# A 192-wide context split as 128 + 64 instead of 128 + 65: one column folded into the weights, and the second part of the weighted sum kept in two halves of the array's columns

## The chip, the cores and the metric

The kernel runs on one core of a Trainium2 chip. The metric is the device time of one execution in microseconds. A core has a matrix engine (TensorE, PE in the profile, with its weight loads shown as PEld), a vector engine (VectorE, DVE), a scalar engine (ScalarE, ACT), GpSimd (POOL) and the queue that issues most of the DMAs (SyncE, SP). Matmul results land in PSUM; ACT and DVE copy them to SBUF. Everything here is in fp32.

## The reference

Cross attention followed by a mixture of experts, for 32 sequences of 100 tokens (256 wide), each with its own context of 361 rows (192 wide). Cut to what matters:

```python
x1 = layernorm(_layernorm(x), ln1_g, ln1_b)         # 32 x 100 x 256
x2 = layernorm(ctx_768, ln2_g, ln2_b)               # 32 x 361 x 192
q, k, v = x1 @ Wq + bq, x2 @ Wk + bk, x2 @ Wv + bv  # 256 wide
attn = softmax(einsum('bqe,bke->bqk', q, k) * 256 ** -0.5)
x = x + einsum('bqk,bke->bqe', attn, v) @ Wo + bo
h = _layernorm(x)
# 31 experts, top 3 of each token, and one shared expert, each 256 -> 256 -> 256 with gelu
x = x + h + shared(h) + sum of gate * expert(h) over the token's three experts
```

A normalised context row, before the gain `ln2_g` and the offset `ln2_b`, is (row - mean) / sigma, so its 192 entries add up to zero (but for rounding). The change rests on this.

## The kernel before, in words

Keys and values are never formed. The query side and the key weights are folded into one 256 x 193 matrix `m_sb` (`fold_scores`, L337), so that the scores of a sequence are `qk` times the normalised context. The 193rd column stands for the constant part of the keys. The weighted sum over keys is taken of the normalised context itself (`weighted`, L523) and only then multiplied by the folded value and output weights `wvo` (`fold_values`, L357, and `project_out`, L539). The context tile `z` has a column of ones behind its 192 columns (`zring`, L137 to L140), which carries the bias row of `wvo` and the softmax denominator.

So the 193 columns (192 and the ones) are worked in two parts, listed as (part, first column, columns) in `AUG` (L304):

```python
C2 = D2 - P            # 64
A2 = C2 + 1            # 65
AUG = [(0, 0, P), (1, P, A2)]
```

The attention is one loop over 32 sequences with some more turns for the lag of later steps (L840 to L935). PE, DVE, ACT, POOL and SP take their instructions in exactly the order in which the loop writes them (`manual_schedule`, L83). In turn i the matrix engine is given, in this order:

- the transposes of the exponentials of sequence i-2 (`exp_transpose`, tile `pe`, L514),
- the scores of sequence i-1 (`scores`, tile `pss`, L495), first the part of 128 context columns, then the part of 65,
- the transposes of a token tile for the router (`route_turn`, tile `pl`, L642),
- the transposes of the context of sequence i (`ctx_transpose`, tile `pz`, L487), three for each part,
- the counts of the router (`route_count`, tile `pp`, L697 and L698),
- the weighted sums of sequence i-2 (`weighted`, tile `pcx`, L528): for each of the two parts three key chunks (128, 128 and 105 keys) are added up in PSUM,
- the router's logits (`pr`, L649), the query projection of a token tile (`token_project`, tile `pq`, L455, the two parts again), a transpose of the next one (`px`, L446) and the output projection (`project_out`, tile `po`, L544).

An fp32 matmul is two instructions on the engine (each with a weight load of its own), a transpose is one. There are 25 token tiles of 128 tokens for 32 sequences, so the steps that go by token tile are missing in some turns. ACT copies each result out: `z2T` (L488), `qk` (L459), `exT` (L515 and L520) and `cT` (L535); DVE takes the row maximum `nm` (L500), and ACT the exponentials `ex` (L506). DVE also normalises the context (L231) and takes its statistics (L246).

Before the loop (the first 15 us), Wq and Wk are transposed on PE (`transposed`, L306, copied by ACT), the seven vectors are turned into columns (`vectors`, L293), two bias columns are made (`bias_cols`, L317), and the folded matrices follow. Wv is transposed in turn 1 and `fold_values` runs in turn 2.

Behind the loop, DVE works out the places of the routed tokens in some thirty small steps (L951 to L1026), while PE does four parts of the shared expert (`shared_mm`, L782); the 92 expert slots follow (`run`, L1167), and a tail that collects and stores the results.

Which part of the 128 x 128 array a matmul uses is worked out from its operands when the program is built: with over 64 rows and over 64 columns of weights it is the full array. With 64 or fewer rows, or columns, it is a tile of 64 (with 32 or fewer, of 32) rows or columns, and the other tiles of the array can then be used by other instructions. The program before has few such places: 64-row tiles in `transposed` and `bias_cols` for Wk and Wv, 32-row tiles in the shared expert's biases (`shared_bias`, L775, and `shared_biases`, L371), and three transposes into 32-column tiles (`p_ec`, L993, and `p_oh`, L997).

Of the kernel before, what the change touches and what calls it, by code (L numbers as in the profile page):

```python
# [15 lines left out]
ET = mybir.EngineType  # L16
PSUM = bass.MemoryType.PSUM


# [19 lines left out]
def xattn_ffn(  # L39
# [18 lines left out]
    C2 = D2 - P  # L58
    A2 = C2 + 1
    DA = D2 + 1  # L60
# [61 lines left out]
    pool.memset(vrows[:8, :], 0.0)  # L122
    pool.memset(vrows[:8, D2:DA], 1.0)

# [48 lines left out]
    load_w(wo_sb, Wo, nc.sync)  # L173
    bo_t = prep_t(1, D1)[:, 0, :]
    nc.sync.dma_start(bo_t[C2:A2, :], bo[None, :])

# [126 lines left out]
    NEC = E // P  # L303
    AUG = [(0, 0, P), (1, P, A2)]  # L304

    def transposed(w_sb, kd, dst, name):  # L306

        rows = sum(m for _, m in kd)
        for ec in range(NEC):
            pt = ps_t(f"pt_{name}{ec}")  # L310
            for c, m in kd:
                nc.tensor.transpose(
                    pt[:, c * P : c * P + m], w_sb[:m, c, ec * P : (ec + 1) * P], ident[:m, :m]
                )
            nc.scalar.copy(dst[:, ec, :rows], pt[:, :rows])

    def bias_cols(w_sb, kd, ln_b, bias, dst, name):  # L317
# [9 lines left out]

    wqT, wkT, wvT = (prep_t(NEC, n) for n in (D1, DA, DA))
    bqc = att.tile([P, NEC], F32, tag="bqc", name="bqc")
    m_sb = att.tile([P, 2, DA], F32, tag="m", name="m_sb")  # L330
# [6 lines left out]
    def fold_scores():  # L337
        for c in range(2):
            pm = ps_m(f"pm{c}")
            for ec in range(NEC):  # L340
                nc.tensor.matmul(
                    pm[:, :DA], wqT[:, ec, c * P : (c + 1) * P], wkT[:, ec, :],
                    start=(ec == 0), stop=(ec == NEC - 1),
                )
            nc.scalar.activation(m_sb[:, c, :], pm[:, :DA], AF.Copy, scale=g1s[:, c : c + 1])
        for c, s, m in AUG:
            pc = ps_m(f"pc{c}")
            for ec in range(NEC):
                nc.tensor.matmul(
                    pc[:m, :1], wkT[:, ec, s : s + m], bqc[:, ec : ec + 1],  # L350
                    start=(ec == 0), stop=(ec == NEC - 1),
                )
            nc.vector.tensor_scalar(
                c_sb[:m, c : c + 1], pc[:m, :1], vcol[:m, c, G2 : G2 + 1], SC, ALU.mult, ALU.mult
            )

    def fold_values():  # L357
        for c, s, m in AUG:
            pw = ps_m(f"pw{c}")
            for ec in range(NEC):  # L360
                nc.tensor.matmul(
                    pw[:m, :D1], wvT[:, ec, s : s + m], wo_sb[:, ec, :],
                    start=(ec == 0), stop=(ec == NEC - 1),
                )
            nc.scalar.activation(wvo[:m, c, :D1], pw[:m, :D1], AF.Copy, scale=vcol[:m, c, G2 : G2 + 1])
        nc.vector.tensor_tensor(wvo[C2:A2, 1, :D1], wvo[C2:A2, 1, :D1], bo_t[C2:A2, :], ALU.add)
        nc.vector.memset(wvo[C2:A2, 1, D1 : D1 + 1], 1.0)

# [34 lines left out]
    transposed(wq_sb, KD1, wqT, "q")  # L403
    transposed(wk_sb, KD2, wkT, "k")
    ctx_stats(0)
    ctx_rough(0)
    vectors()
    for t in XG[0]:
        token_stats(t)
    token_rough(0)  # L410
    bias_cols(wq_sb, KD1, B1, BQ, lambda ec: bqc[:, ec : ec + 1], "bqc")
    bias_cols(wk_sb, KD2, B2, BK, lambda ec: wkT[:, ec, D2:DA], "bkc")
    ctx_rstd(0)
    token_rstd(0)
# [35 lines left out]
    def token_project(t):  # L450
# [7 lines left out]
        for c, s, m in AUG:  # L458
            nc.scalar.activation(  # L459
                qk[:m, c, t * P : (t + 1) * P], pq[:m, c * P : (c + 1) * P], AF.Identity,  # L460
                bias=c_sb[:m, c : c + 1], scale=vcol[:m, c, G2 : G2 + 1],
            )
# [60 lines left out]
    def weighted(b):  # L523
        z, exT = ztile.pop(b), att_eT.pop(b)
        for a, s, m in AUG:
            pw = ps_m(f"pcx_{b}_{a}")
            for c, (_, n) in enumerate(CH):
                nc.tensor.matmul(  # L528
                    pw[:m, :L1], z[:n, c, s : s + m], exT[:n, c, :], start=(c == 0), stop=(c == NCH - 1)
                )  # L530
            q = 0
            while q < L1:
                col = (b * L1 + q) % RING
                n = min(L1 - q, RING - col)
                nc.scalar.copy(cT[:m, a, col : col + n], pw[:m, q : q + n])  # L535
                q += n


    def project_out(t):  # L539
        k, j = divmod(t, TPB)  # L540
        xt = xb[k][:, j, :]
        po = ps_m(f"po_{t}")
        for a, _, m in AUG:
            nc.tensor.matmul(  # L544
                po[:, : D1 + 1], cT[:m, a, t * P % RING : t * P % RING + P], wvo[:m, a, :], start=(a == 0), stop=(a == 1)
            )
# [293 lines left out]
    for i in range(B + 5):  # L840
# [80 lines left out]
        if i == 1:  # L921
            transposed(wv_sb, KD2, wvT, "v")
            bias_cols(wv_sb, KD2, B2, BV, lambda ec: wvT[:, ec, D2:DA], "bvc")
# [13 lines left out]
    shared_half(1, 1, ps_m)  # L937
    for t in range(2):
        shared_mm(t)
# [65 lines left out]
    for t in range(2):  # L1005
        shared_add(t)
    shared_mm(2)
    PACK, BITS = 4, 5
# [287 lines left out]
```

## Time and profile before

| what | value |
|---|---|
| time, median of 3 runs | 476.42 us (474.83 to 476.57) |
| time of the profiled execution | 475.09 us |
| its span, first to last instruction | 473.2 us |
| attention loop, first scores to last scores | 17.1 to 211.8 us, so 6.28 us a turn |
| experts and tail | from about 240 us on |
| PE busy over the span | 451.0 us (95%) |
| DVE, ACT, POOL busy | 311.0 (66%), 252.3 (53%), 254.0 us (54%) |

The busy time of PE in the profile counts each matmul from its issue to the modelled end of its results, and matmuls overlap in the pipeline; what one costs is better read from the distance between the starts of two that follow each other. In the timeline rows below, the columns are the start in us from the start of the span, the time that the row covers, the engine, the line, the operation, output<-inputs, the shape (rows*columns of the array in front), and the number of instructions that were merged into the row. A row that was asked for with a narrow window holds only the instructions in that window.

### The profile page before, as it was taken

The page shows a single profiled execution, that of the slowest core. Times are in us where ns is not written, and L with a number is a line of the kernel's source. Part 1 is how long each engine was busy: PE and PEld are TensorE (multiplying, and loading weights), DVE is VectorE, ACT ScalarE, POOL GpSimd, SP SyncE. Part 2 cuts the span into 40 slices and gives each one's busy share as a digit, 9 for nine tenths or more (in the row PEclk, how much of TensorE's full clock was granted, in tenths as well). Part 3 has the DMA queues.
Part 4 walks back from the last instruction along what each step waited for, and adds up shares of the span by engine and source line. Part 5 has one row for each costly group of instructions (what it writes and reads, how often), then busy time and mean ns, then how long its engine had stood idle before and what let it go on. Part 6 is the DMA issues. An engine that isn't in the chain of part 4 may idle for free. (4 is left out here: it accounts for less than half of the span.)

```text
span 473.2 us, 10916 instructions
## 1 busy us (share of the span) xinstructions
PE 451.0 (95%) x2978; PEld 389.2 (82%) x2978; DVE 311.0 (66%) x1273; ACT 252.3 (53%) x839; POOL 254.0 (54%) x523
## 2 busy tenths in 40 slices
PE   8899999898999999999799999999999999999996
PEld 8687887777888788887478999999999999997564
DVE  2679998998999896867764444444444455655177
ACT  2565877787877787774514444444444444443210
POOL 6322486887676757575803555554655555556200
PEclk9979999999999999999999999999999999999999
DMA  6987954454545741021269988898798899962593
GB/s 188 272 223 216 278 168 126 140 161 148 160 130 155 230 165 65 35 82 58 91 181 289 317 257 253 264 274 256 239 279 269 268 365 353 355 247 71 185 408 131
DMA packets 65863, 98.79 MB, mean 209 GB/s; under 512 B 8289, under 2 KB 40616, under 8 KB 65800
## 3 DMA queue, kind: packets, MB, share of 16 engines
q1 hardware_dynamic: 56360, 72.60, 51.6%
q0 software_dynamic: 8768, 24.79, 13.8%
q8 instruction: 28, 0.46, 0.4%
q10 hardware_dynamic: 672, 0.66, 0.4%
q14 instruction: 35, 0.29, 0.2%
HBM read 68.27 MB, written 29.74 MB: 207 GB/s over the span
## 5 line engine op out<-in xcount | busy, mean ns | idle before, releaser
L566 POOL DMA_INDIRECT y_d<-ys,yrow x92 | 90.3, 982 | 96.2 <-ACT ys L1139 42.4
L1123 ACT ACTIVATE hT<-ph,b1t 128x128 f32<-128x128 f32 x184 | 57.6, 364 | 102.6 <-issue 53.2
L1118 PE MATMUL ph<-xgT,w 128*128 128x128 f32 x736 | 101.9, 282 | 1.0 <-DVE xgT L1110 1.0
L1118 PEld LDWEIGHTS ph<-xgT,w 128*128 128x128 f32 x736 | 94.7, 197 | 1.5 <-DVE xgT L1110 1.4
L1133 PE MATMUL py<-w2r,hT 128*128 x368 | 94.3, 380 | 0.0
L566 POOL DMA_INDIRECT xs_d<-xl,su x75 | 75.1, 1002 | 30.7 <-ACT cT L535 13.0
L1133 PEld LDWEIGHTS py<-w2r,hT 128*128 128x128 f32 x368 | 62.9, 190 | 4.8
L1141 DVE TENSOR_SCALAR ys<-py,gate 128x256 f32<-128x256 f32 x46 | 22.3, 484 | 61.3 <-PE py L1133 40.8
L1110 DVE COPY xgT<-pg 128x256 f32<-128x256 f32 x92 | 38.1, 420 | 28.0 <-PE pg L1108 28.0
L495 PE MATMUL pss<-z2T,qk 65*100 65x361 f32 (+1 forms) x128 | 46.2, 483 | 0.8 <-ACT qk L459 0.6
L528 PE MATMUL pcx<-exT,z 128*65 128x100 f32 (+3 forms) x384 | 45.3, 268 | 0.0
L528 PEld LDWEIGHTS pcx<-exT,z 128*65 128x65 f32 (+3 forms) x384 | 40.6, 168 | 0.7 <-ACT er L675 0.7
L1108 PEld LDWEIGHTS pg<-ident,xg 128*128 128x128 f32 x184 | 35.4, 195 | 4.2
L1108 PE MATMUL pg<-ident,xg 128*128 128x128 f32 x184 | 35.5, 277 | 0.0
L246 DVE BATCH_NORM_STATS2 stc<-z 128x6 f32<-128x192 f32 (+1 forms) x96 | 27.8, 345 | 7.0 <-DMA z<-in_ctx_dram 7.0
L455 PE MATMUL pq<-zT,m_sb 128*128 128x128 f32 (+1 forms) x200 | 28.2, 284 | 2.1 <-DVE eq L711 1.2
L544 PE MATMUL po<-wvo,cT 128*128 128x257 f32 (+1 forms) x100 | 27.4, 394 | 2.7 <-ACT cT L535 2.4
L506 ACT ACTIVATE ex<-pss,nm 100x361 f32<-100x361 f32 x32 | 18.0, 563 | 20.6 <-DVE nm L500 17.1
L495 PEld LDWEIGHTS pss<-z2T,qk 65*100 65x100 f32 (+1 forms) x128 | 19.2, 170 | 11.2 <-ACT qk L459 1.5
L1139 ACT ACTIVATE ys<-py,gate 128x256 f32<-128x256 f32 x46 | 21.8, 475 | 11.7 <-issue 8.8
L487 PE MATMUL pz<-ident,z 128*128 128x128 f32 (+2 forms) x192 | 26.2, 271 | 1.1 <-PE pss L495 0.9
L487 PEld LDWEIGHTS pz<-ident,z 128*128 128x128 f32 (+2 forms) x192 | 22.4, 143 | 5.1 <-PE pss L495 1.5
(242 smaller groups left out, 826.1 us busy)
## 6 DMA issues: line engine op xcount, KB each, us to landing
w<-in_L_ffn_We_dram SPq DMA_DIRECT2D x92, 256.0 KB
xg<-xs_d SPq DMA_DIRECT2D x92, 131.5 KB
w2r<-in_L_ffn_We_dram SPq DMA_DIRECT2D x31, 256.0 KB
z<-in_ctx_dram SPq DMA_DIRECT2D x32, 192.0 KB
y<-y_d SPq DMA_DIRECT2D x13, 384.0 KB
ye<-y_d SPq DMA_DIRECT2D x12, 384.0 KB
xs_d<-none SPq DMA_DIRECT2D x3, 1052.0 KB
x<-in_x_dram SPq DMA_DIRECT2D x5, 512.0 KB
```

What stands on the lines that cost most here:

```text
L246: nc.vector.bn_stats(st[:n, c, :], ztile[b][:n, c, :D2])
L455: nc.tensor.matmul(pq[:m, c * P : (c + 1) * P], m_sb[:, d, s : s + m], z[:, d, :], start=(d == 0), stop=(d == 1))
L487: nc.tensor.transpose(pt[:m, ks : ks + n], z[:n, c, s : s + m], ident[:n, :n])
L495: nc.tensor.matmul(pss[:L1, :L2], qk[:m, a, b * L1 : (b + 1) * L1], z2T[:m, a, :], start=(a == 0), stop=(a == 1),)
L528: nc.tensor.matmul(pw[:m, :L1], z[:n, c, s : s + m], exT[:n, c, :], start=(c == 0), stop=(c == NCH - 1))
L544: nc.tensor.matmul(po[:, : D1 + 1], cT[:m, a, t * P % RING : t * P % RING + P], wvo[:m, a, :], start=(a == 0), stop=(a == 1))
L566: ins = nc.gpsimd.indirect_dma_start(out=dst, out_offset=bass.IndirectOffsetOnAxis(ap=index, axis=0), in_=src, in_offset=None).ins
L1108: nc.tensor.transpose(pt[:, c * P : (c + 1) * P], g[:, c::2], ident)
L1110: nc.vector.tensor_copy(xgT[i].rearrange("p c s -> p (c s)"), pt[:, : 2 * P])
L1118: nc.tensor.matmul(ph[:, f * P : (f + 1) * P], w1s[:, c, f::2], z[:, c, :], start=(c == 0), stop=(c == 1))
L1123: nc.scalar.activation(hT[i][:, f, :], ph[:, f * P : (f + 1) * P], AF.Gelu, bias=b1t[:, f, i : i + 1])
L1133: nc.tensor.matmul(py[:, :D1], h[:, f, :], w2f[:, bass.ds(e * (2 * D1) + f * D1, D1)], start=(f == 0), stop=(f == 1),)
```

## The change

Because a normalised row adds up to zero, its first entry is minus the sum of the others. A product with a vector w over 192 columns is therefore a product with w - w[0] over the last 191. So the first context column is dropped from every product and put into the weights: `with_gains` multiplies Wk and Wv by `ln2_g`, `without_first` transposes and subtracts the first column. The 191 columns and the ones make 192 = 128 + 64, and `AUG` becomes `[(0, 1, 128), (1, 129, 64)]`.

With 64 columns the second part fits into half of the array's columns. In `weighted` its key chunks 0 and 2 are added up on PSUM partitions 0 to 63 and chunk 1 on partitions 64 to 127. `cT` and `wvo` then have 128 rows for the second part too, `wvo` with the same 64 rows twice, so that `project_out` adds the two halves. The bias row of `wvo` goes in through an extra matmul of one row (`last_row`, `bo_t`). One part of the shared expert (`shared_mm(2)`) moves from behind the router's placement steps to in front of them.

In the program that this makes, the following use a tile of the array instead of the whole: the second part of `pz` (3 transposes a turn), of `pq` (4 instructions for a token tile) and of `pcx` (6 instructions a turn) use 64-column tiles, of `pcx` one key chunk in the upper one; the second part of `pss` (4 instructions a turn) uses a 64-row tile. The order of the steps in the loop is the same, and the order of SP's DMAs is unchanged.

```diff
-    pool.memset(vrows[:8, D2:DA], 1.0)
...
-    bo_t = prep_t(1, D1)[:, 0, :]
-    nc.sync.dma_start(bo_t[C2:A2, :], bo[None, :])
+    bo_t = prep_t(2, D1).rearrange("p n c -> p (n c)")
+    nc.sync.dma_start(bo_t[:1, :D1], bo[None, :])
+    pool.memset(bo_t[:1, D1 : D1 + 1], 1.0)
+    pool.memset(bo_t[:1, D1 + 1 : D1 + C2], 0.0)
+    pool.memset(bo_t[:1, D1 + C2 : D1 + C2 + 1], 1.0)
+    last_row = bo_t[:1, D1 + 1 : D1 + 1 + C2]
...
-    AUG = [(0, 0, P), (1, P, A2)]
+    AUG = [(0, 1, P), (1, 1 + P, C2)]
...
+    def with_gains(w_sb, dst):
+        for c, m in KD2:
+            nc.vector.tensor_scalar(dst[:m, c, :], w_sb[:m, c, :], vcol[:m, c, G2 : G2 + 1], None, ALU.mult)
+
+    def without_first(w_sb, dst, name):
+        for ec in range(NEC):
+            pt = ps_t(f"pt_{name}{ec}")
+            for c, m in KD2:
+                nc.tensor.transpose(
+                    pt[:, c * P : c * P + m], w_sb[:m, c, ec * P : (ec + 1) * P], ident[:m, :m]
+                )
+            nc.vector.tensor_copy(dst[:, ec, :1], pt[:, :1])
+            nc.vector.tensor_scalar(dst[:, ec, 1:D2], pt[:, 1:D2], dst[:, ec, :1], None, ALU.subtract)
...
     def fold_values():
...
+        pw = ps_m("pw1")
+        for h in range(2):
+            half = pw[h * C2 : (h + 1) * C2, :]
+            nc.tensor.matmul(half[:, : D1 + 1], last_row, bo_t[:1, : D1 + 1], start=True, stop=False)
             for ec in range(NEC):
                 nc.tensor.matmul(
+                    half[:, :D1], wvT[:, ec, 1 + P : DA], wo_sb[:, ec, :], start=False, stop=(ec == NEC - 1)
                 )
-        nc.vector.tensor_tensor(wvo[C2:A2, 1, :D1], wvo[C2:A2, 1, :D1], bo_t[C2:A2, :], ALU.add)
-        nc.vector.memset(wvo[C2:A2, 1, D1 : D1 + 1], 1.0)
+        nc.scalar.copy(wvo[:, 1, :], pw[:, : D1 + 1])
...
     transposed(wq_sb, KD1, wqT, "q")
-    transposed(wk_sb, KD2, wkT, "k")
     ctx_stats(0)
     ctx_rough(0)
     vectors()
+    with_gains(wk_sb, wkg)
...
     bias_cols(wk_sb, KD2, B2, BK, lambda ec: wkT[:, ec, D2:DA], "bkc")
+    without_first(wkg, wkT, "k")
...
                 qk[:m, c, t * P : (t + 1) * P], pq[:m, c * P : (c + 1) * P], AF.Identity,
-                bias=c_sb[:m, c : c + 1], scale=vcol[:m, c, G2 : G2 + 1],
+                bias=c_sb[:m, c : c + 1],
...
         for a, s, m in AUG:
             pw = ps_m(f"pcx_{b}_{a}")
             for c, (_, n) in enumerate(CH):
+                h = c % 2 if a else 0
+                last = c + (2 if a else 1) >= NCH
                 nc.tensor.matmul(
-                    pw[:m, :L1], z[:n, c, s : s + m], exT[:n, c, :], start=(c == 0), stop=(c == NCH - 1)
+                    pw[h * C2 : h * C2 + m, :L1], z[:n, c, s : s + m], exT[:n, c, :], start=(c == h), stop=last
                 )
...
-                nc.scalar.copy(cT[:m, a, col : col + n], pw[:m, q : q + n])
+                nc.scalar.copy(cT[:, a, col : col + n], pw[:, q : q + n])
...
-        for a, _, m in AUG:
+        for a in range(2):
             nc.tensor.matmul(
-                po[:, : D1 + 1], cT[:m, a, t * P % RING : t * P % RING + P], wvo[:m, a, :], start=(a == 0), stop=(a == 1)
+                po[:, : D1 + 1], cT[:, a, t * P % RING : t * P % RING + P], wvo[:, a, :], start=(a == 0), stop=(a == 1)
             )
...
         if i == 1:
-            transposed(wv_sb, KD2, wvT, "v")
+            with_gains(wv_sb, wvg)
+            without_first(wvg, wvT, "v")
...
-    for t in range(2):
+    for t in range(3):
         shared_mm(t)
...
-    shared_mm(2)
```

## The prediction, made before the changed kernel had run

> **What bounds the kernel now.** I read the page first, for the engine that is full, then busy time by window over the attention loop, because only the loop and what stands ahead of it are changed, then PE's timeline of one turn, and last PE's waits there.
>
> ```profile
> PE 451.0 (95%) x2978; PEld 389.2 (82%) x2978; DVE 311.0 (66%) x1273; ACT 252.3 (53%) x839; POOL 254.0 (54%) x523
> PEclk9979999999999999999999999999999999999999
> ...
> 45.00:70.00 25.00, 24.28 (x180) 20.50 (x179) 23.47 (x112) 19.00 (x70) 14.21 (x30) 1.00 0.85 227
> 120.00:145.00 25.00, 23.96 (x178) 20.41 (x176) 23.30 (x105) 18.99 (x72) 17.48 (x33) 1.00 0.48 142
> ...
> 57.84 1.46 PE L495 MATMUL pss<-z2T,qk 128*100 128x361 f32 x4
> 59.14 0.39 PE L642 MATMUL pl<-ident,xl 128*128 128x128 f32 x2
> 59.36 0.79 PE L487 MATMUL pz<-ident,z 128*128 128x128 f32 x6
> 59.99 0.32 PE L697 MATMUL pp<-sums,onesf 128*128 128x31 f32 x2
> 60.17 1.41 PE L528 MATMUL pcx<-exT,z 128*128 128x100 f32 x12
> 61.42 0.55 PE L649 MATMUL pr<-wr,qk 128*128 128x31 f32 x4
> ```
>
> In the windows the columns are the length, then busy us of PE, PEld, DVE, ACT and POOL, the granted clock, the DMA share and GB/s. PE is at 24 of 25 us at full clock, DVE close behind at 23.4, ACT at 19. From start to start in the turn at 57.84: four score instructions take 1.30 us, of which the first pays for its own weights, so about 302 ns each; six transposes take 0.63 us, 108 ns each; the twelve of pcx take 1.25 us. The single starts show two speeds in these twelve: 112 ns in the first part (128-column weights) and 86 ns in the second (65 columns). So a weight load of 128 columns takes about 107 ns, and 100 moving columns about 84 ns, and each instruction costs the longer of the two, since the next load runs beside the matmul. For 64 columns I put the load at 54 ns, half of 107; for 100 columns at 84.
>
> PE's waits, from the view of who waits for whom between 40 and 215 us (total, times, longest):
>
> ```profile
> PEld po L544 <- ACT cT L535: 5.0, 10, 1.2
> PEld pr L649 <- ACT ex L506: 4.5, 5, 1.1
> PEld pq L455 <- DVE eq L711: 1.4, 2, 0.7
> ```
>
> With four smaller ones for pq (issue 0.7, ex 0.4, pr 0.3) and some for pss and pz, PE waits about 17 us of 175. PE is the bound, with some 0.6 us of waiting in a turn of 6.28 us.
>
> **The change: what a tile of the array costs.** The program before changes between the whole array and a part of it in few places, and they show the price:
>
> ```profile
> 9.64 0.30 PEld L322 LDWEIGHTS bkc<-vcol,w2r 128*128 128x128 f32 x2
> 9.96 0.29 PEld L322 LDWEIGHTS bkc<-vcol,w2r 64*128 64x128 f32 x2
> 10.27 0.30 PEld L322 LDWEIGHTS bkc<-vcol,w2r 128*128 128x128 f32 x2
> ...
> 441.58 0.59 PE L750 MATMUL phs<-qk,ws_sb 128*128 128x512 f32 x1
> 442.10 0.18 PEld L780 LDWEIGHTS pys<-b,gT 32*128 32x128 f32 x1 [0.75 <-issue]
> ...
> 50.92 0.38 PE L544 MATMUL po<-wvo,cT 65*128 65x257 f32 x1
> 51.23 0.31 PEld L374 LDWEIGHTS pb<-ident,b1r 32*128 32x128 f32 x2 [0.33 <-PE po L544]
> ```
>
> Loads of one kind in bqc and bkc follow each other at 112 ns, so a pair takes 0.22 us; each pair here takes 0.31 to 0.32, since the next pair is on another tile. At 441.58 the 512 columns stream for 428 ns (the distance of those matmuls), to 442.01; the load for the 32-row tile starts at 442.10, 90 ns later, where elsewhere it starts beside the matmul. At 50.92: 257 columns, 216 ns, to 51.14; load at 51.23, again 90 ns. Leaving a tile shows the same (pys to 442.66, next load 442.75). The transposes of Wv (23.03 and 23.29) leave 46 ns. So at a change of tile nothing overlaps: matmul, a pause D of 90 ns (46 between transposes), load, matmul. The cost of one change is the last matmul + D + the next load, less the longer of matmul and load.
>
> [...]
>
> In each turn, in ns:
> - pss, second part, 64-row tile, between 361-column matmuls: in, 90 + 84 = 174; out to pl or pz, 90 + 107 = 197. 371 x 32 turns = 11.9 us.
> - pz, second part, 64-column tile: in, 88 + 46 + 54 - 88 = 100; out to pp or pcx, 88 + 46 + 107 - 107 = 134. 234 x 32 = 7.5 us.
> - pcx: in, 84 + 90 + 54 - 84 = 144; out to pr, pq or px, 84 + 90 + 107 - 107 = 174. 318 x 32 = 10.2 us. The two column halves can overlap: the four 32-row tiles of pys start 7 ns apart (the starts from 442.11), each with its own load. Chunk 1 then runs beside chunks 0 and 2, so 4 x 86 instead of 6 x 86: minus 172 x 32 = 5.5 us.
> - pq, by token tile: in, 107 + 90 + 54 - 107 = 144; out, 197. 341 x 25 = 8.5 us.
>
> Sum: 11.9 + 7.5 + 10.2 - 5.5 + 8.5 = 32.6 us of PE time. No row shows a change from the whole array to a column tile and back that isn't hidden in a wait; the nearest is p_oh, a 32-column tile, whose successor's load came 81 ns after its stream. So I price column tiles as row tiles; the bounds are 0 (then only pss's 11.9 - 5.5 = 6.4 us remains) and the 90 ns taken.
>
> Do transposes in a column tile stay single? [...] The two p_ec transposes, with one weight column and so in such a tile, start at 234.43 and 234.54, 108 ns apart like whole ones. [...]
>
> **What the waits take back.** The time is put ahead of pr, pq and po, and these wait now for ACT and DVE work that starts earlier on PE (ex after pss, cT after pcx). Their waits, 5.0 + 4.5 + 2.8 = 12.3 us in 175, are 14 us in the loop's 200. All of it at most, none at least; I take 13, since the switches out of pss and in pz, some 0.4 us, come between pss and pr, and pq's 0.34 ahead of po. DVE doesn't take over: it has some 5.9 us of work in a turn that grows to 6.9. Loop: 32.6 - 13 = +19.6 us.
>
> **Ahead of the loop.** wkT was ready at 11.36 (last bkc sum). Now PE turns the vectors first, DVE scales Wk (two of 256 columns, 433 ns each by the L231 row of that shape), bias sums end near 10.8, the four transposes of Wk (0.95 us before) come behind them, and DVE does two copies of a column (158 ns, the L326 row) and two subtractions of 191 columns from PSUM (about 0.4, below the 484 of the 256-column L549). fold_scores starts near 12.3 instead of 11.1. Behind these on DVE wait the statistics' factors and the normalising of context 0, so ACT's first zx moves too: +1.0 us, none if the turns at 8.6 us that follow absorb it. Wv in turn 1: two scalings and four small steps, 2 us of DVE where ACT had two copies; fold_values gets two one-row matmuls of 257 columns (four instructions of 215 ns), a second set of 64 columns, and changes of tile, less a DVE add (0.4) that waited 2.4: together +1.0, from 0 to 3.
>
> **Costed at nothing.** cT for 128 rows (both row counts take 234 to 247 ns), po with 128 rows (216 ns apart either way), qk without a scale (ACT has 6 us idle in 25, and ACT's 457 ns don't change), three POOL memsets (0.1 us each, POOL is done with its set-up by 5.9 and wanted at 8.2), SP's queue (no DMA is added or moved). shared_mm(2), 4 x 215 ns, leaves the place behind the biases, where the next PE step waits for ACT's ohT (ended 238.25), and enters PE's 0.8 us of waiting ahead of p_ec at 234.43: delay of p_ec up to 0.3, and its reader eT waited until 237.9 for pys. Nothing; at most 0.3 either way.
>
> **The sum.** 19.6 + 2 = +21.6 on the profiled execution's 475.1 (span 473.2 and 1.9 around it): 496.7. That execution is 1.3 us below the median of 476.42, within the spread shown. I say 496.
>
> **The rivals.**
> A, above, 0.74: every change of tile drains. from +12 us (the pauses of column tiles at half, 6.6 us less, all 14 us of waits taken back, no set-up) to +33 (no wait taken back): 487 to 508.
> B, 0.12: only row tiles drain, column tiles change for nothing. 11.9 - 5.5 + 2, less what the waits take: -3 to +8, so 473 to 483, near 477. For it: no clean row of a column tile. [...]
> C, 0.08, faster: the drains fall into PE's waits altogether. 3.8 round trips of a turn cost less than what the waits take (13/32 = 0.41) and the halves give (0.17), less set-up 0.06: it decides at 0.52/3.8 = 140 ns for a round trip. With none priced, the 5.5 us of the halves remain: about 471. Against: the cheapest round trip above, bkc's, is already 0.18, and pss's 0.37.
> D, 0.06: the change doesn't do what it says; the halves don't overlap (+5.5) or transposes there double (+10). 502 to 515.
>
> **How the numbers follow.** Half a per cent, 2.4 us, is about what a measurement of this kernel can tell from no change. Slower: nearly all of A and D and a third of B, 0.83. Same: half of B and a sliver of A, 0.07. Faster: C and some of B, 0.10. The range for 8 in 10 is 480 to 508: it leaves out C, most of B and the upper half of D, 0.2.
>
> **What would show it.** In the profile after: turns of about 6.9 us instead of 6.28; PE starts 170 to 200 ns further apart at pss's second part and behind it, 100 to 150 at the second parts of pz, pcx and pq, with the next weight load behind the matmul's stream; chunk 1 of pcx starting within some 20 ns of chunk 0; the waits for ex and cT nearly gone. I am wrong if loads into column tiles start beside the last matmul of the whole array, or if the waits stay beside longer PE work (then up to 508).

## The result, and the profile after

The changed kernel takes 494.89 us (median of 6 runs, 493.40 to 495.57), the kernel before 475.62 us beside it (6 runs, 472.46 to 477.14): a ratio of 1.0414, 95% interval 1.0370 to 1.0459. The prediction had said slower, 496 us. The total is right; where the time sits is not where the prediction put it. Ratios here and below are of undisturbed executions; one profile, that of `filled`, was taken of a disturbed one, and no time is read from it.

The profiled execution took 495.5 us, span 493.7. First the page of the changed kernel: busy time by engine, and the granted clock in 40 slices of the span.

```profile
PE 476.7 (97%) x2986; PEld 385.7 (78%) x2986; DVE 314.9 (64%) x1283; ACT 247.3 (50%) x835; POOL 252.3 (51%) x525
PEclk9666999999999999999989999999999999999999
```

PE has 25.7 us more busy time for eight more instructions; the other engines are within 5 us of what they had. In the clock row three slices (12.3 to 49.4 us) stand at 6 where before they stood at 9, 7 and 9. This is the first sign of something the prediction has no term for. The 7 of the kernel before is a stretch at half clock too, in turns 1 and 2; its windows there show a clock of 0.53 and 0.62:

```profile
24.00:28.00 4.00, 4.00 (x13) 2.79 (x13) 3.81 (x21) 2.78 (x9) 0.36 (x2) 0.53 1.00 198
28.00:32.00 4.00, 4.00 (x25) 3.86 (x24) 3.58 (x18) 2.19 (x6) 2.33 (x4) 0.62 1.04 343
```

Next the busy time by window, columns as before (length, PE, PEld, DVE, ACT, POOL, clock, DMA share, GB/s): first one stretch in the middle of the loop of the changed kernel, then all turns from the third scores to the last, of the kernel before and of the changed one.

```profile
120.00:145.00 25.00, 25.00 (x174) 18.69 (x172) 22.46 (x102) 19.87 (x75) 17.45 (x35) 1.00 0.48 142
```

```profile
34.46:211.82 177.36, 168.43 (x1236) 143.06 (x1234) 154.15 (x689) 137.49 (x505) 116.55 (x235) 1.00 0.50 150
```

```profile
47.96:232.44 184.48, 183.44 (x1235) 134.90 (x1234) 153.99 (x683) 133.82 (x505) 114.52 (x233) 1.00 0.46 143
```

The middle stretch holds 174 PE instructions where the kernel before had 178, and PE stands nowhere in it. Over the 29 turns PE's idle time fell from 8.9 us (177.36 - 168.43) to 1.0, and the turns grew by 7.1 us, 6.12 to 6.36 us each. That is a third of the whole difference. The 177.35 of the kernel before is on the long side: in the profiles of `mm2`, `wide_before`, `warm_before` and `warm_two` below, whose loop is the same, these turns take 175.6 to 176.6 us, while `gains_top`, `wide_after` and `warm_after`, with the changed loop, take 184.4 to 184.5. So the change costs 7 to 9 us in these turns. The starts of the scores split the span:

| us of the profiled execution | before | after | difference |
|---|---|---|---|
| start to first scores | 17.08 | 20.42 | +3.3 |
| turns 1 and 2 | 17.38 | 27.54 | +10.2 |
| 29 turns, third to last scores | 177.35 | 184.48 | +7.1 |
| last scores to the end | 261.43 | 261.27 | -0.2 |

So 13.5 us of the 20.5 arise in the first 48 us. Now the timeline of one turn of the changed kernel, PE alone, to set beside the turn at 57.84 of the kernel before:

```profile
59.51 1.55 PE L522 MATMUL pss<-z2T,qk 128*100 128x361 f32 x4
60.99 0.51 PE L672 MATMUL pl<-ident,xl 128*128 128x128 f32 x2
61.33 0.79 PE L514 MATMUL pz<-ident,z 128*128 128x128 f32 x6
61.96 1.32 PE L558 MATMUL pcx<-exT,z 128*128 128x100 f32 x12
63.20 0.63 PE L679 MATMUL pr<-wr,qk 128*128 128x31 f32 x4
63.67 1.27 PE L482 MATMUL pq<-zT,m_sb 128*128 128x128 f32 x8
```

From start to start the scores take 1.48 us (1.30 before) and the pl behind them 0.34 (0.22). The six transposes pz take 0.63 us, exactly what they took before, though three of them are in the 64-column tile. The twelve of pcx take 1.24 us against 1.25.

The single starts give the price of a change of tile, in the form in which the prediction worked it out:

| per turn, ns | at the way in | at the way out | sum | predicted |
|---|---|---|---|---|
| pss (second part 64 rows) | 91 + 82 | 92 + 111 | 376 | 371 |
| pz (second part 64 columns) | 0 | 0 | 0 | 234 |
| pcx (halves of columns) | 92 + 53 | 91 + 81 | 317 | 318 |
| pq (64 columns) | 94 + 51 | 94 + 56 | 295 | 341 |

Each pair is the excess of two starts that follow each other over what the same two take without a change, the pause and then the load that nothing covers; the medians over all turns from 50 us on agree within 5 ns. In pcx chunk 1 starts 7 ns behind chunk 0 (62.712 and 62.719), and the six instructions of the second part take four steps.

Who waits for whom, PE alone from 48 to 210 us, of the changed kernel:

```profile
PE po L574 <- ACT cT L565: 0.6, 1, 0.6
PE pz L514 <- ACT qk L673: 0.2, 1, 0.2
```

PE's waits for ex (3.5 us in that window before) and for eq (1.2) are gone and that for cT is halved (1.2 before), much as the prediction said. Last the timeline of turn 1 in the changed kernel: one line of PE, and the DVE line that it waits for.

```profile
29.62 1.45 PE L332 MATMUL pt_v<-ident,w2r 128*128 128x128 f32 x4 [5.29 <-DVE w2r L325]
31.00 2.12 PE L343 MATMUL bvc<-vcol,w2r 128*128 128x1 f32 x8
```

```profile
29.06 0.18 DVE L211 BATCH_NORM_AGGREGATE mv<-st_x 128x2 f32<-128x6 f32 x1
29.16 0.57 DVE L325 TENSOR_SCALAR w2r<-w2r,vcol 128x256 f32<-128x256 f32 x2
```

PE stands 5.29 us ahead of the transposes of Wv, because `with_gains(wv_sb, wvg)` is queued on DVE behind the statistics of contexts and tokens of that turn. Before, these transposes took Wv as it had been loaded.

### The profile page after: what moved, and what is told of

It reads as the page before. It is cut to its first block, busy times and chain, and to the rows that moved or that the text cites. A ratio compares the mean times of both kernels' runs of the same rounds, so it can differ in the third digit from the quotient of the medians.

```text
span 493.7 us, 10936 instructions
## 1 busy us (share of the span) xinstructions
PE 476.7 (97%) x2986; PEld 385.7 (78%) x2986; DVE 314.9 (64%) x1283; ACT 247.3 (50%) x835; POOL 252.3 (51%) x525
## 5 line engine op out<-in xcount | busy, mean ns | idle before, releaser
L522 PE MATMUL pss<-z2T,qk 64*100 64x361 f32 (+1 forms) x128 | 51.3, 500 | 0.0
L558 PE MATMUL pcx<-exT,z 128*64 128x100 f32 (+3 forms) x384 | 44.6, 278 | 0.0
L558 PEld LDWEIGHTS pcx<-exT,z 128*64 128x64 f32 (+3 forms) x384 | 36.5, 167 | 3.6 <-ACT nmr L702 0.4
L482 PE MATMUL pq<-zT,m_sb 128*128 128x128 f32 (+1 forms) x200 | 33.7, 302 | 0.0
L522 PEld LDWEIGHTS pss<-z2T,qk 64*100 64x100 f32 (+1 forms) x128 | 16.6, 168 | 17.7 <-issue 7.4
L527 DVE TENSOR_REDUCE nm<-pss 100x1 f32<-100x361 f32 x32 | 16.9, 528 | 19.5 <-PE pss L522 17.2
L574 PE MATMUL po<-wvo,cT 128*128 128x257 f32 x100 | 27.1, 394 | 0.9 <-ACT cT L565 0.6
L482 PEld LDWEIGHTS pq<-zT,m_sb 128*128 128x128 f32 (+1 forms) x200 | 24.9, 172 | 4.0 <-issue 0.4
L514 PE MATMUL pz<-ident,z 128*128 128x128 f32 (+2 forms) x192 | 27.2, 278 | 0.2 <-ACT qk L673 0.2
```

What stands on the lines that cost most here:

```text
L482: nc.tensor.matmul(pq[:m, c * P : (c + 1) * P], m_sb[:, d, s : s + m], z[:, d, :], start=(d == 0), stop=(d == 1))
L514: nc.tensor.transpose(pt[:m, ks : ks + n], z[:n, c, s : s + m], ident[:n, :n])
L522: nc.tensor.matmul(pss[:L1, :L2], qk[:m, a, b * L1 : (b + 1) * L1], z2T[:m, a, :], start=(a == 0), stop=(a == 1),)
L558: nc.tensor.matmul(pw[h * C2 : h * C2 + m, :L1], z[:n, c, s : s + m], exT[:n, c, :], start=(c == h), stop=last)
L574: nc.tensor.matmul(po[:, : D1 + 1], cT[:, a, t * P % RING : t * P % RING + P], wvo[:, a, :], start=(a == 0), stop=(a == 1))
```

## The experiments

Times are given as the ratio to the kernel before, run beside each, with its 95% interval. Stretches, and lengths of half clock, are of the one profiled execution of each kernel. "29 turns" is third to last scores: 177.35 before, 184.48 after.

The letters of the theories are each expectation's own. The first four runs ask how much of the difference is the stand in turn 1, and how much the changes of tile between matmuls, which cost PE a pause and an uncovered load.

**Wv's gains at the top of turn 1** (`gains_top`)

```
         if i == 1:
-            with_gains(wv_sb, wvg)
             without_first(wvg, wvT, "v")
...
+        if i == 1:
+            with_gains(wv_sb, wvg)
         for b in ...:       # loads of contexts, the first thing in the turn
```

> The changed kernel, with the two scalings of Wv (with_gains) at the top of turn 1 instead of at its end, so that DVE does them before its statistics and the matrix engine finds them ready. Theory A (the trace of after): PE waits 5.3 us for them in turn 1, falls to half clock behind that, and turns 1 and 2 cost some 10 us more than before; then this gives back 5 to 10 us: 485 to 490. Theory B (the prediction: set-up costs 2 us, the rest is changes of array tile in the loop): 0 to 1 us back, 494.

1.0402 (1.0353 to 1.0451): the ratio lies inside the changed kernel's interval; by the medians (493.04 and 494.89 us) 1.9 us less. The wait of 5.29 us is gone (PE now waits 1.0 for z2T there) and turn 1 takes 9.25 us, yet turn 2 still takes 14.51. Busy time by window in this kernel shows why:

```profile
24.00:28.00 4.00, 4.00 (x15) 3.01 (x15) 3.87 (x20) 2.53 (x8) 0.21 (x1) 0.57 1.09 219
28.00:32.00 4.00, 4.00 (x14) 2.57 (x14) 3.39 (x17) 1.57 (x4) 2.19 (x3) 0.50 1.05 341
32.00:36.00 4.00, 4.00 (x20) 3.03 (x20) 2.48 (x14) 1.06 (x5) 1.10 (x3) 0.50 0.35 94
36.00:40.00 4.00, 4.00 (x13) 1.91 (x12) 0.00 (x0) 0.95 (x3) 0.00 (x0) 0.72 0.06 21
```

PE is busy all 16 us, at half clock for (0.43 + 0.50 + 0.50 + 0.28) x 4 / 0.5 = 13.7 us of them. Taking the wait away left turn 2 at half clock. The 5 to 10 us that theory A expected from it did not come.

**Idle matmuls in the wait of turn 1** (`filled`)

```
         if i == 1:
             with_gains(wv_sb, wvg)
+            fill = ps_m("fill")
+            for _ in range(24):
+                nc.tensor.matmul(fill[:, :P], ident, ident, start=True, stop=True)
             without_first(wvg, wvT, "v")
```

> The changed kernel, with 24 matmuls of the identity (results unused, some 5.1 us at full clock) put ahead of the transposes of Wv in turn 1, where PE waits for DVE. The wait stays, only PE has work in it. Theory A1 (much of the loss in turns 1 and 2 is the clock that falls in the wait): turns from there on run at full clock, 4 to 6 us back, 489 to 491. Theory A2 (the wait alone costs): nothing back, 495, or up to 5 us lost if the fill runs at half clock. Theory B: nothing.

1.0362 (1.0308 to 1.0416): between the two expectations, and its interval overlaps the changed kernel's, so the time decides nothing. The granted clock does: it was 0.978 to 0.986 in five of its six executions, above all six of the changed kernel (0.966 to 0.977). Work in the wait does keep the clock up; some 2.5 us of time came of it by the ratios.

**Scores on the whole array** (`scores_full`)

```
-                pss[:L1, :L2], qk[:m, a, b * L1 : (b + 1) * L1], z2T[:m, a, :],
+                pss[:L1, :L2], qk[: m + a, a, b * L1 : (b + 1) * L1], z2T[: m + a, a, :],
```

A 65th row of zeros puts the second part on 65 rows, so that it uses the whole array: in the kernel before, the 65-row part starts 303 ns behind the 128-row part and pl 303 ns behind it, where the 64-row part of the changed kernel has 395 and 394.

> The changed kernel, with one row of zeros added to the second part of the scores (65 rows instead of 64), so that these four matmuls of a turn use the whole array; all else as in after. The price of the two changes of tile there is 373 ns of PE a turn by the trace of after, 11.9 us in 32 turns. Theory B (what the waits take back was small, 13 us of 32.6): 9 to 12 us back, 483 to 486. Theory A (in the 29 turns from the third on, after is only 7.1 us longer than before, since waits took back about 0.5 us a turn of 0.75; with 0.37 less, the rest hides in the waits): about 7 us back, 487 to 489.

1.0283 (1.0229 to 1.0336). The 29 turns take 179.26 us, 5.2 less than with all tiles. The pause and loads are 376 x 29 = 10.9 us of PE; about half comes back as time and half goes into waits that return. By the ratios it is 6 us less than the changed kernel, near the 7 of theory A.

**Both halves of pcx in one half** (`one_half`)

```
-                h = c % 2 if a else 0
-                last = c + (2 if a else 1) >= NCH
+                h = 0
+                last = c + 1 == NCH
```

> The changed kernel, with all three key chunks of the second part of the weighted sums in the lower column half (partitions 0 to 63), the upper half of that part's sums left at zero; nothing can overlap. If the halves do overlap, the second part takes 6 x 86 ns again instead of 4 x 86: 172 ns a turn, up to 5.5 us, so 497 to 500; if PE's time is only half visible, 2 to 3 us. If the overlap in the trace is only in the records: no difference, 495.

1.0505 (1.0458 to 1.0553). The 29 turns take 188.74 us, 4.3 more: the two halves do run beside each other, and save 4.3 of the 5.0 us (172 ns x 29) that four steps in place of six can save. Rival D, that the halves don't overlap, falls.

The next four ask what holds the clock down, and what is left without tiles.

**No matmul tile at all** (`all_full`; gains early, scores as above, pq and pcx with 65 columns, pcx in one accumulation)

```
-                    pw[h * C2 : h * C2 + m, :L1], z[:n, c, s : s + m], exT[:n, c, :], ...
+                    pw[: m + a, :L1], z[:n, c, s : s + m + a], exT[:n, c, :], ...
```

> The changed kernel with Wv's gains at the top of turn 1 and with every matmul tile of the loop widened to the whole array: scores with 65 rows (a row of zeros), pq and pcx with 65 weight columns, pcx without its two halves; only the transposes of pz keep their 64-column tile. What is left of the change is the set-up (vectors turned ahead of the biases, Wk and Wv scaled and less their first column, fold_values in two sets of columns). Theory A (changes of tile between matmuls cost the loop its 7 us, transposes change for nothing): the 29 turns from the third score on take 177 us as before, against 184.5. If the half clock of turns 1 and 2 belongs to the set-up alone, the third score still starts at about 41 us and the time is 481 to 484; if the pauses at the tiles hold the clock down, it starts near 36 and the time is 475 to 478. Rival (pz's change of tile does cost its 234 ns a turn): the 29 turns take 181 us or more.

1.0120 (1.0080 to 1.0161), 13 us below `gains_top`. From the third scores to the last it takes:

```profile
37.17:212.82 175.65, 168.40 (x1235) 144.25 (x1234) 152.59 (x683) 133.42 (x505) 115.06 (x233) 0.99 0.50 151
```

175.65 us, 8.8 less than with all tiles, with PE's busy time where it was before any change (168.4); it is also what the loop of the kernel before takes in `mm2`, `wide_before` and `warm_two`. The 64-column tile of pz is still in this kernel and costs nothing that can be seen; the rival (181 or more) falls. The other part of the gain is in the clock. Its windows over turns 1 and 2:

```profile
24.00:28.00 4.00, 3.15 (x16) 2.29 (x17) 3.22 (x19) 3.29 (x10) 0.65 (x1) 0.88 1.07 213
28.00:32.00 4.00, 4.00 (x25) 3.24 (x24) 3.86 (x18) 1.32 (x4) 2.38 (x4) 0.69 1.08 344
```

Half clock for (0.12 + 0.31) x 4 / 0.5 = 3.4 us, where `gains_top`, with the same set-up but with tiles, has 13.7. The third scores start at 37.17 us instead of 41.47, close to the "near 36" that was expected if the pauses at tiles keep the clock down. The two profiles exaggerate it: ahead of the loop `all_full` had 10.2 us at half clock and `gains_top` 3.4, so that in all it is 13.7 against 17.1 us. The table behind the runs has all executions.

**Only the halves of pcx in a tile** (`sp_full`: as `all_full`, pcx as in the changed kernel)

> The changed kernel with Wv's gains early and with whole-array scores and pq, so that the halves of pcx are the only matmul tiles left in the loop. Against the kernel with no matmul tile, a turn has 318 - 172 = 146 ns more PE work (4.7 us over 32 turns). Theory A (the waits for ex and cT, 0.6 us a turn, hide it): the 29 turns from the third score on take 176 to 178 us (175.7 without tiles, 184.5 with all). Theory clock, half (pauses at tiles hold the clock down after it fell): the half clock behind 26 us lasts between the 5 us without tiles and the 13 us with all, turns 1 and 2 take 17 to 20 us; altogether 1.010 to 1.020 times the kernel before. Rival (the pair in two halves gives nothing, and its changes go on top): 180 us or more for the 29 turns, ratio above 1.02.

1.0099 (1.0058 to 1.0140), the same as `all_full` within the intervals. The 29 turns take 177.09 us, 1.4 above `all_full`, of 145 ns x 29 = 4.2 us of PE work: the waits hide two thirds. Half clock behind 26 us for 10.2 us, between the 3.4 and the 13.7, as expected. But this profile has the lowest clock (0.969) of the six executions behind the ratio, and their mean of 0.980 is above `all_full`'s 0.976, so that the part about the clock is not shown.

**Wide bias sums, in the changed kernel** (`wide_after`, gains early) **and in the kernel before** (`wide_before`)

```
-                    pb[:, :1], ..., vcol[:m, c, ln_b : ln_b + 1],
+                    pb[:, :P], ..., vcol[:m, c, ln_b : ln_b + 1].to_broadcast([m, P]),
```

The one-column matmuls of bqc, bkc and bvc stream their column 128 times; only the first column of the sum is read.

> The changed kernel with Wv's gains at the top of turn 1, and in the bias sums bqc, bkc and bvc each one-column matmul streams that column 128 times (weights and loads unchanged, only the first column of the sum is read). Theory clock (the stretch of one-column sums counts as an idle PE, and the clock falls behind it): the half clock behind 26 us goes or shortens from 13 us to under 4, turn 2 takes 9 to 11 us instead of 14.5, the time is 487 to 490. Rival (the waits and the pauses at the tiles pull the clock down, whatever the sums are): turn 2 stays at 14 to 15 us, the time within 1 us of the kernel with Wv's gains early, 492 to 494.

> The kernel before with the same one edit: one-column matmuls of the bias sums stream their column 128 times. Theory clock: the half clock from 24.6 to 31.4 us goes, and perhaps that from 10.5 to 13.8; 2 to 5 us less than before, 470 to 473. Rival: the clock falls all the same, or the waits for DVE and ACT in turns 0 to 2 take the place: within 1 us of before.

1.0318 (1.0272 to 1.0365), some 4 us below `gains_top`; and 0.9965 (0.9939 to 0.9992), 1.7 us below the kernel before. In both profiles the half clock behind 10 us (3.4 us of it in `gains_top` and in the kernel before) is gone. That behind 24 us is as long as without the edit: 13.7 us in `wide_after`, with turn 2 at 14.49 us, and 6.8 in `wide_before`. So each theory got half: short sums lower the clock in the first place, and in the second it falls behind this stand of PE (`wide_after`):

```profile
23.25 0.53 PE L332 MATMUL pt_v<-ident,w2r 128*128 128x128 f32 x2 [1.05 <-ACT z2T L515]
```

It does not always: two of the 14 executions of `wide_before` were granted a clock of 1.000, so they had next to no half clock.

**One part of the change alone** (`mm2`: the kernel before with shared_mm(2) early)

```
-    for t in range(2):
+    for t in range(3):
         shared_mm(t)
...
-    shared_mm(2)
```

> The kernel before with one part of the change alone: shared_mm(2) ahead of shared_gelu(1) instead of behind the biases. The prediction costed it at nothing, at most 0.3 us either way: the same time as before. Rival: it delays p_ec and with it the choice of the tokens behind it, up to its own 0.86 us.

1.0006 (0.9990 to 1.0022). It costs nothing, as the prediction said. It shows something else as well. Up to the end of the loop this is the program before, instruction for instruction, and yet its half clock lay elsewhere: 10.2 us from 9.9 us and 3.4 from 27.0, where the profile of the kernel before has 3.4 from 10.6 and 6.8 from 24.2. One window of each, the kernel before first:

```profile
14.00:16.00 2.00, 2.00 (x22) 1.94 (x21) 1.46 (x7) 1.47 (x4) 0.00 (x0) 1.00 1.09 286
```

```profile
14.00:16.00 2.00, 2.00 (x13) 2.00 (x14) 1.13 (x5) 0.81 (x3) 0.00 (x0) 0.50 1.08 285
```

The first scores came at 19.04 us instead of 17.08, and turns 1 and 2 took 14.80 us instead of 17.38. So differences of 2 to 3 us between two profiles in the first 35 us can be chance.

**Idle matmuls where PE stands a microsecond** (`warm_after`: as `wide_after`; `warm_before`: as `wide_before`; both with five of 256 columns between the two sets of transposes of Wv)

```
         for ec in range(NEC):
+            if name == "v" and ec:
+                fill = ps_m("fill")
+                for _ in range(5):
+                    nc.tensor.matmul(fill[:, :E], ident, wq_sb[:, 0, :], start=True, stop=True)
             pt = ps_t(f"pt_{name}{ec}")
```

> The changed kernel with Wv's gains early, wide bias sums and the same five idle matmuls. Theory pause: the half clock from 24.8 to 38 us goes, turn 2 takes 8 to 10 us instead of 14.5, the third score starts at about 35 us instead of 41.2, the time is 480 to 482, a ratio near 1.02: what is left is the 7 us of the 29 turns and some 2 of the set-up. Rival: the clock falls all the same, turn 2 stays at 14 to 15, the ratio near 1.032.

> The kernel before with wide bias sums and with five idle matmuls of 256 columns (1.08 us at full clock) in the 0.93 us in which PE waits between the two sets of transposes of Wv in turn 1. Theory pause: that stand, behind which the clock fell 2.2 us later in three kernels, is what lowers it; without it the half clock from 23.8 to 31 us goes, some 3 us less than with wide sums alone, 6 to 7 thousandths below the wide kernel, ratio about 0.99 to before. Rival: the clock falls all the same (the transposes and short sums around it count as little): the time of the wide kernel, ratio 0.996 to 0.999.

1.0223 (1.0190 to 1.0256) and 0.9944 (0.9919 to 0.9968). The same windows as above, in `warm_after`:

```profile
24.00:28.00 4.00, 4.00 (x20) 3.07 (x19) 3.27 (x19) 2.89 (x8) 0.60 (x1) 1.00 1.04 206
28.00:32.00 4.00, 4.00 (x28) 2.65 (x27) 3.62 (x16) 1.50 (x5) 2.40 (x4) 1.00 1.06 333
32.00:36.00 4.00, 4.00 (x26) 2.54 (x22) 3.01 (x19) 2.18 (x8) 1.09 (x3) 1.00 0.38 95
```

The clock stays at full, turn 2 takes 9.35 us instead of 14.49, and the ratio falls by 0.0095, 4.5 us. Theory pause holds in that filling the stand of 1.05 us for z2T takes the half clock away. Whether it is the stand or the little work in these microseconds that lowers the clock this pair can't say, since the idle matmuls change both; the last section comes back to it. A step of the expectation was off: each fp32 matmul of 256 columns is two instructions of 215 ns, so five took 2.2 us instead of 1.08, and in `warm_before` turn 1 grew by 1.0 us.

**A version that beats both kernels** (`warm_two`: `warm_before` with two idle matmuls instead of five)

> The kernel before with wide bias sums and two idle matmuls (four instructions of 215 ns, 0.86 us) where PE waits 0.93 us; five took 2.2 us, 1.1 more than the wait. Theory pause: 0.86 us of work in the stand is enough, the clock stays at full behind it, turn 1 (first to second scores) is 1.1 us shorter than with five (8.3 instead of 9.4 us), the ratio to before is about 0.992. Rival: the shorter work leaves enough of a stand for the clock to fall, turn 2 is again 8 to 9 us instead of 6.2, the ratio is that of the wide sums alone, 0.9965.

468.99 us, the kernel before 471.62 beside it: 0.9947 (0.9928 to 0.9966). Its timeline of PE, and its clock row:

```profile
20.47 0.47 PE L316 MATMUL pt_v<-ident,w2r 128*128 128x128 f32 x2
20.87 1.13 PE L313 MATMUL fill<-w2r,ident 128*128 128x256 f32 x4
21.87 0.53 PE L316 MATMUL pt_v<-ident,w2r 128*128 128x128 f32 x2
```

```profile
PEclk9999999899999999999899999999999999999998
```

The stand is filled, the clock is at full from 8 us through turn 2, turn 1 takes 8.31 us and turn 2 6.23 (8.57 and 8.81 before). The turns are those that theory pause expected (8.3 and 6.2); the ratio is short of its 0.992, its interval overlaps that of the wide sums alone, and that two are better than five the ratios (0.9947 and 0.9944) don't show. That it beats the kernel before is shown.

**The granted clock of all executions.** Since the half clock of one profile is partly chance, here is the mean clock over the span for the executions behind the ratios. A hundredth is some 4.8 us of PE's clock; the time lost to it is at most that, as PE doesn't always bound the kernel.

| kernel | executions | mean clock (lowest to highest) |
|---|---|---|
| before, beside `gains_top` | 10 | 0.982 (0.973 to 0.991) |
| changed | 6 | 0.971 (0.966 to 0.977) |
| `filled` | 5 | 0.982 (0.978 to 0.986) |
| `gains_top` | 6 | 0.969 (0.963 to 0.975) |
| `scores_full`, `one_half` | 5, 6 | 0.973 (0.967 to 0.978), 0.973 (0.967 to 0.977) |
| `all_full` | 6 | 0.976 (0.973 to 0.980) |
| `sp_full` | 6 | 0.980 (0.969 to 0.987) |
| `mm2` | 22 | 0.981 (0.976 to 0.989) |
| `wide_after`, `wide_before` | 6, 14 | 0.985 (0.981 to 0.994), 0.990 (0.983 to 1.000) |
| `warm_after`, `warm_before`, `warm_two` | 6, 14, 6 | 0.994, 0.995, 0.994 (0.987 to 1.000) |

The wide sums (0.969 to 0.985) and the idle matmuls (0.985 to 0.994) raise the clock over all executions, not only in the profiles. The tiles together lower it, from 0.976 to 0.969, some 4 us at most; with the tiles of the scores alone taken out (`scores_full`, 0.973) no difference from the changed kernel is shown.

## Why the prediction was right, and where it was not

The direction and the size were right: 496 said, 494.9 measured. The mechanism that it rested on is there, at its price. But the sum came out through two terms that were wrong by about the same amount in opposite senses, and that is luck: with the loop's term alone put right it would have said 485 to 487.

- **Price of a change between matmuls: right.** 376 ns for pss (371 said), 317 for pcx (318), 295 for pq (341: its way out came to 150 instead of 197). In all three a change of tile shows as a pause of 91 to 94 ns and a load that nothing covers (51 to 111 ns).
- **The pz term: wrong.** "234 x 32 = 7.5 us" was worked out from the row-tile pause and the 46 ns of the transposes of Wv. Measured: 0. The start behind the way in is 93 ns from the last whole one, and so is the first of pcx behind it. These transposes show no pause; the ones into row tiles, from which the price was taken, do pause (46 ns for Wv, 90 for pb). The choice "So I price column tiles as row tiles" was right for matmuls in column tiles and wrong for transposes in them. That the transposes stay single instructions was right (three for each part, 93 to 112 ns apart); that they double, the +10 us of rival D, is shown by no run.
- **The halves: right.** Seven ns apart, four steps in place of six, and `one_half` loses 4.3 of 5.0 us without them.
- **What the waits take back: somewhat too small.** Over the 29 turns the measured prices come to 10.9 (pss) + 4.2 (pcx less the halves) + 6.5 (22 turns of pq) = 21.6 us of PE. The turns grew by 7.1 in the pair of profiles, up to 8.8 against the other profiles of the same loop, so 12.8 to 14.5 were taken back. (PE's idle time by the records fell by less, 7.9 us, as a matmul counts as busy to its modelled end.) The prediction's 13 for 32 turns is 11.8 for 29. It knew of 17 us of waits.
- **The loop: +19.6 said, +7.1 to +8.8 in 29 turns measured, which is +7.8 to +9.7 for 32.** The turns are 6.36 us, not the 6.9 that were to show. Most of what is missing is the pz term (7.5); the rest is pq (1.2) and the waits.
- **Ahead of the loop and in its first two turns: +2 said, +13.5 measured in the profiles.** This is the other term that failed. The work itself was not far off. At full clock the first scores start 1.1 us later (`wide_after` 17.05, `wide_before` 15.97; +1.0 said). Turns 1 and 2, at full clock and both with five idle matmuls, take 18.06 us in `warm_after` and 15.52 in `warm_before`, so +2.5 (+1.0 said, and 0.5 of it belongs to the tiles). Together that is an estimate of 3.6 us. The other 10 us are the clock and the wait for Wv's gains. This pair of profiles makes the clock's part too large: by their granted clocks (0.987 and 0.967) the two lost 6.1 and 16.4 us of PE's clock, 10.3 apart, while the means of the table are 5.9 apart. As an estimate of the 19.3 us between the medians: 8 to 10 the loop, 3.6 the work of the set-up, 6 at most the clock, 2 the wait (`gains_top`). The prediction took the moves of DVE's work into account only as work: it didn't ask what stands ahead of `with_gains(wv_sb, wvg)` in DVE's queue, and it read the turns of 8.6 us before the loop settles as slack, where they were turns at half clock (6.8 us of it). The page had shown that, as the 7 in its clock row.

- **Costed at nothing: not contradicted.** shared_mm(2) was tried alone and costs nothing. cT and po with 128 rows, the scale left out and the memsets were not tried alone; in `all_full`, which keeps them but for the rows of cT that it fills with zeros, PE's busy time in the 29 turns is that of the kernel before. DVE didn't take over: 22.5 of 25 us, PE 25.

Of the rivals, B (column tiles free, 477 us) names the half that is true of transposes. C needed a round trip below 140 ns; the cheapest of the three that cost anything is 295. D fell with `one_half` and with the transposes of pz, which did not double.

That the tiles together lower the clock is shown by all executions of `gains_top` and `all_full`, which have the same set-up: 0.969 and 0.976. Which tiles do it is not: `sp_full`, with those of pcx alone, has 0.980. How they do it is open too. What the set-up alone still costs beyond `all_full`'s 1.0120 was not taken apart further.

## What to carry to other kernels

Price a part of the array by where it lies in PE's stream: each excursion of a matmul into a tile of 64 rows or columns and back cost some 300 to 375 ns here, more than the one halved load saves (the load behind the way in took 51 to 53 ns for 64 columns; the prediction's rows give about 107 for 128), while transposes went into a tile of 64 columns and back for nothing; one further row or column that keeps the whole array was cheaper (175.65 us for the 29 turns in `all_full`, 184.48 in the changed kernel). Read the clock row ahead of the loop before costing a set-up: in the profiles a stand of a microsecond was followed by 3.4 to 13.7 us at half speed, and four idle matmul instructions in the stand kept the clock at full. Judge the clock by many executions, since one program had its half clock in different places in two profiles. When a total comes out right, split it by stage all the same; here a loop term 10 to 12 us too large stood against a set-up term 11.5 us too small.

## What the runs showed of the hardware that was not expected

- **Half clock comes in whole steps of 3.41 us.** In the profiles the stretch behind 24 us lasted 3.4 us in `all_full` and `mm2`, 6.8 in the kernel before and in `wide_before`, 10.2 in `sp_full`, 13.7 in `gains_top` and `wide_after`, 17.1 in the changed kernel and in `scores_full`: one to five times 3.41. The stretches at full clock between two at half are whole steps too, 10.24 us in the kernel before (13.98 to 24.22) and 6.83 in the changed one (20.63 to 27.46), so that in these two profiles the changes lie on a grid of 3.41 us. Up to five steps passed before the clock returned, with PE busy by the records all the time (but for waits of 2.2 us in the changed kernel and 3.5 in `scores_full`); and the clock fell behind a stand of 1.05 us in `wide_after` and `all_full`, in `mm2` even behind two of 0.29 and 0.39 us.
- **What came ahead of a fall is a step in which PE streamed little.** On this grid I added up the moving columns of each step, at 0.837 ns a column at full clock (361 columns take 302 ns), from 7 us, where the clock's records begin, to 225 us in the profiles of the kernel before and of the changed one. Of the steps at full clock, four were followed by half clock; in these PE streamed for 0.14 and 0.33 of the time (before) and for 0.07 and 0.03 (changed). In the 111 others it was 0.45 or more but for one of 0.40. That joins the two places: the step of 0.14 has the one-column sums in it, and behind 10 us the half clock is gone in `wide_before`; that of 0.33 has the stand among short work (0.92 us there), and behind 24 us the half clock is gone in `warm_two`. In `mm2`, the same program up to the end of the loop, the changes lie at 9.92, 20.17, 27.00 and 30.42 us, so that its grid lies some 0.65 us earlier than that of the kernel before; that its half clock lay elsewhere for this reason is an estimate. This was read from the traces afterwards, and no run was made to try it. What brings the clock back it doesn't say: at half clock, with the columns at twice the time, steps of 0.76 to 0.93 came ahead of a return and steps of up to 0.87 ahead of none.
- **Sums of one column lower the clock too.** With the weights loaded as before, streaming the column 128 times took the half clock behind 10 us away in both wide kernels (`wide_after` and `wide_before`; 3.4 us in `gains_top` and in the kernel before). In `warm_after`, with the same sums, there was half clock from 12.6 to 19.4 us all the same, where PE had waited 1.1 us for the vectors.
- **A transpose went into a 64-column tile and out of it for nothing** (93 to 94 ns from start to start on either side, as in the kernel before, whose 65 columns are on the whole array), while a matmul paid 91 to 94 ns and its load.
